# Macaron block with fp4 feed-forward: the last 64 features of the down product as a doubled float32r split

## Chip, cores and metric

One core of a Trainium2 chip. The metric is device time in microseconds of one execution of the whole program, median of repeated runs.

## What is computed

The input has 8 x 1024 tokens of 256 features, 8192 tokens in all. Six sublayers follow each other, each with a layer norm ahead of it and a residual sum behind it: fp4 feed-forward, attention with decay, fp4 feed-forward, ternary feed-forward, attention with memory, ternary feed-forward. The change lies in the fp4 feed-forward alone, which runs twice with the same weights:

```python
def fp4_quant_dequant(x):                      # blocks of 16 along the last dim
    xb = x.reshape(shape[:-1] + (shape[-1] // BLOCK, BLOCK))
    scale = jnp.maximum(jnp.max(jnp.abs(xb), axis=-1, keepdims=True) / 6.0, 1e-12)
    xn = xb / scale
    idx = jnp.searchsorted(_MID, jnp.abs(xn))
    return (_GRID[idx] * jnp.sign(xn) * scale).reshape(shape)

def fp4_linear(x, w):
    return jnp.einsum('bsk,nk->bsn', fp4_quant_dequant(x), fp4_quant_dequant(w))

gate = fp4_linear(x, w_gate)                   # 256 -> 704
y = fp4_linear(x, w_up)                        # 256 -> 704
h = jax.nn.silu(gate) * y
return fp4_linear(h, w_down)                   # 704 -> 256
```

## The kernel before

**Tiles.** Tokens are worked on in 64 tiles of 128 (`NT`), four to a group (`G`), 16 groups. The residual stream `X` stays on the chip for the whole program. `ffn_fp4(prepare, after)` is one fp4 stage. It runs `for i in range(NT + 3)`, a software pipeline by hand: iteration i makes the gate and up products of tile i, rounds tile i-1, multiplies the turned tile i-3 by its scales, and makes the down product of tile i-4.

**Order.** Nearly every instruction passes through `pin`, which ties it behind the instruction pinned before it on the same engine. So each engine runs in program order by itself, and instructions of different engines are held apart only by their data and by buffers that have to come free.

**One tile i, engine by engine.**
- PE: for each half q, two products of `pg` (gate) and two of `pu` (up), 128x352 each, in `products` (L861); the transpose `pts` of the scales of tile i-1 (L891) between `pg` and `pu` of the second half; then the down product `po` of tile i-4 (`down`, L960).
- ACT: silu of `pg` (L871), the copy of a scale (`copies`, L815) and the magnitudes of h (L821), the copy of the turned scales `sct` (L897).
- DVE: the rounding of tile i-1 to the fp4 grid (`round_grid`, L886: one instruction back into h, one that writes the grid values in bfloat16 into `gd`), the gate times up of tile i (`gated`, L876), the block maxima and reciprocals of `scale` (L804, L806, L811), layer norm statistics of the coming stage, the residual sum of `po` (L969).
- POOL (GpSimd): h times the reciprocal scales (`scale`, L817), and `multiplied` (L927): the turned grid of tile i-3 (`gt`) times its scales, which a DMA has spread into `ht`; in every second iteration also the normalized x of a coming group (`xt`), handled in the same way.
- SP issues the DMAs: `sd` takes the turned scales to memory (L899), `gt` is the DMA transpose of `gd` (L912), `ht` and `xt` spread the scales from `sd` (L904), `gtx` is the transpose of the rounded x (L1084).

There is one `gd`, two `gt`, one `sct`, and five `ht` in the first stage, four in the second. `pu` and `po` have one PSUM buffer each.

**The down product.** 704 features are five chunks of 128 and one of 64 (`DCH`, `NC` = 6). `ht` is [128, 6, 128] and `wd` [128, 6, 256], both float32; the unused 64 rows of the last chunk are zero, in `wd` and in `gd`. `down` makes six float32 products into `po`:

```python
for c in range(NC):
    kn = tail if c == NC - 1 else P
    pin(nc.tensor.matmul(po, lhsT=ht[:kn, c, :], rhs=wd[:kn, c, :],
                         start=(c == 0), stop=(c == NC - 1)))
```

**Weights and ends.** `w_down` is quantized during the first iterations of the first stage (`prep_down_scale`, `prep_down`) and turned in iteration 5 (`prep_down_turn`, L643 and L647), ahead of the first down product. The last two tiles of a stage don't go by DMA: `turn` (L948, L950) transposes h on PE in three groups of chunks, 4, 1 and 1, and ACT copies each group to `ht`.

**Elsewhere.** The ternary stages make their products from two float32r factors, a rounded high part and a remainder (`xh`, `xl` at L1193; `hh`, `hl` at L1220), against weights that stand as float32r.

Of the kernel before, what the change touches and what calls it, by code (L numbers as in the profile page):

```python
# [9 lines left out]
F32 = mybir.dt.float32  # L10
F32R = mybir.dt.float32r
BF16 = mybir.dt.bfloat16
I32 = mybir.dt.int32
AF = mybir.ActivationFunctionType
ALU = mybir.AluOpType
# [3 lines left out]
P = 128  # L19
D = 256  # L20
# [3 lines left out]
G = 4  # L24
# [10 lines left out]
FP4_TIE = 1.0 + 2.0**-22  # L35
# [4 lines left out]
def macaron_kernel(  # L40
# [25 lines left out]
    nc = tc.nc  # L66
    NB, S, _ = x.shape
# [3 lines left out]
    NI = w_gate.shape[0]  # L71
# [5 lines left out]
    DCH = [(k, min(P, NI - k)) for k in range(0, NI, P)]  # L77
# [365 lines left out]
    def turned_part(xt, k):  # L443
        return xt.rearrange("p (j k) t -> p k j t", k=2)[:, k]

    wd = w_f0.tile([P, NC, D], F32, name="wd")
    nc.gpsimd.memset(wd[DCH[-1][1] :, NC - 1, :], 0.0)
    with (
        tc.tile_pool(name="prep_ps", bufs=2, space=PSUM, side="right") as prep_ps,
        tc.tile_pool(name="prep_pq", bufs=1, space=PSUM, side="right") as prep_pq,  # L450
# [184 lines left out]
    def prep_down(c):  # L635
        fp4_round(wd_n[:, c, :], wd_sc.pop(c), raw, nc.gpsimd, pin)

    def prep_down_turn(ps, tag):
        for i, (k0, kn) in enumerate(DCH):
            pt = ps.tile([P, D], F32, tag=tag, name="ptd")  # L640
            for c in range(2):
                pin(
                    nc.tensor.transpose(  # L643
                        pt[:kn, c * P : (c + 1) * P], wd_n[:, c, k0 : k0 + kn], ident
                    )
                )
            pin(nc.scalar.copy(wd[:kn, i, :], pt[:kn, :]))  # L647


    def load_a0():  # L650
# [116 lines left out]
    def ffn_fp4(prepare, after):  # L767
        with ExitStack() as st:
# [10 lines left out]


            gd = gp.tile([P, NC * P], BF16, name="gd")
            nc.gpsimd.memset(gd[:, NI:], 0.0)
            scales = []
            for n in range(2):
                sc = gp.tile([P, P], F32, name=f"sc_{n}")
# [11 lines left out]
            DOWN = 5  # L797
            HT_BUFS = DOWN if prepare else 4

            def scale(v, pool, at, mul=nc.gpsimd, sc=None):  # L800
                vb = v.rearrange("p (b k) -> p b k", k=16)
                _, nb, _ = vb.shape
                am, sp = qp[:, at : at + nb], qp[:, at + nb : at + 2 * nb]
                pin(nc.vector.tensor_reduce(am, vb, AX.X, ALU.max, apply_absolute_value=True))  # L804
                pin(
                    nc.vector.tensor_scalar(  # L806
                        sp, am, -FP4_TIE / 6.0, -1e-12 * FP4_TIE, ALU.mult, ALU.min
                    )
                )
                rs = pool.tile([P, nb], F32, tag="q_rs", name="q_rs")  # L810
                pin(nc.vector.reciprocal(rs, sp))  # L811
                if sc is None:
                    sc = pool.tile([P, nb], F32, tag="q_sc", name="q_sc")
                copies.append(
                    lambda: pin(nc.scalar.activation(sc, sp, AF.Copy, scale=-1.0 / FP4_TIE))  # L815
                )
                pin(mul.tensor_tensor(vb, vb, rs[:, :, None].to_broadcast([P, nb, 16]), ALU.mult))  # L817
                return sc

# [61 lines left out]
            def by_dma(i):  # L881
                return 0 <= i < NT - 2

            def round_grid(v, mg, grid):
                for op, dst in ((ALU.add, v), (ALU.subtract, grid)):
                    pin(nc.vector.scalar_tensor_tensor(dst, mg, FP4_LEAST, v, ALU.max, op))  # L886
# [38 lines left out]
            def multiplied(wide, grid):  # L925
# [4 lines left out]
                    )  # L930
                )

            def scaled_turn(i):
                hs.pop(i)
                ht = spreading.pop(i)
                multiplied(ht, turning.pop(i))
                hts[i] = (ht, P)

            def turn(i):
                h, _ = hs.pop(i)  # L940
                ht = hp.tile([P, NC, P], F32, tag="ht", name="ht", bufs=HT_BUFS)
                for c0, c1 in ((0, 4), (4, 5), (5, 6)):
                    kn = DCH[c0][1]
                    pa = ps_t.tile([P, 4, P], F32, tag="pt", name="pt")
                    for c in range(c0, c1):
                        k0 = DCH[c][0]
                        pin(
                            nc.tensor.transpose(pa[:kn, c - c0, :], h[:, k0 : k0 + kn], ident)  # L948
                        )
                    pin(nc.scalar.copy(ht[:kn, c0:c1, :], pa[:kn, : c1 - c0, :]))  # L950
                hts[i] = (ht, DCH[-1][1])

            def down(i, ps=ps_o, tag="po"):
                g, j = divmod(i, G)
                ht, tail = hts.pop(i)
                po = ps.tile([P, D], F32, tag=tag, name="po")
                for c in range(NC):
                    kn = tail if c == NC - 1 else P
                    pin(
                        nc.tensor.matmul(  # L960
                            po,
                            lhsT=ht[:kn, c, :],
                            rhs=wd[:kn, c, :],
                            start=(c == 0),
                            stop=(c == NC - 1),
                        )
                    )
                pin(
                    nc.vector.scalar_tensor_tensor(  # L969
                        X[g][:, j, :], po, 0.5, X[g][:, j, :], ALU.mult, ALU.add  # L970
                    )
                )
# [38 lines left out]
            for i in range(NT + 3):  # L1011
                g, j = divmod(i, G)
                h = hp.tile([P, NI], F32, tag="h", name="h") if i < NT else None
                if i == 0 and not prepare:
                    xts[0], copied = turn_products(xts[0])
                    copied()
                pts = None
                for q in range(2):
                    if i < NT:
                        pg = ps_h.tile([P, NHALF], F32, tag="pg", name="pg", bufs=1)  # L1020
                        if q == 0:
                            pu = ps_h.tile([P, 2, 512], F32, tag="pu", name="pu", bufs=1)
                            sg = hp.tile([P, 2, NHALF], F32, tag="sg", name="sg", bufs=1)
                        products(i, q, 0, pg)
                        if q == 1 and i == 3:
                            xts[1], copied = turn_products(xts[1][0])
                        if prepare and late_weights and q == 1:
                            late_weights.pop()(ps_t)
                        if q == 1 and by_dma(i - 1):
                            pts = scales_turned(i - 1)  # L1030
                        products(i, q, 1, pu[:, q, 0:NHALF])
                        silu(sg, q, pg)
                        if i == NT - 1:
                            gated(h, sg, pu, slice(q, q + 1))
                        elif q:
                            gated(h, sg, pu, slice(0, 2))
                    if q == 0:
                        while copies and i < NT:
                            copies.pop(0)()
                    elif i == 3:  # L1040
                        copied()

                    if 0 < i < NT and q == 0:
                        magnitudes(hs[i - 1][0], qp[:, 0:NI])
                        if by_dma(i - 1):
                            round_grid(hs[i - 1][0], qp[:, 0:NI], gd[:, :NI])
                    if i == NT - 1:
                        if q == 1:
                            round_(*hs[i - 1], qp[:, 0:NI])

                        part = h[:, q * NHALF : (q + 1) * NHALF]
                        at = NI + q * NHALF // 8
                        mul = nc.vector if q else nc.gpsimd
                        halves.append((part, scale(part, hp, at, mul)))
                    if i == NT:
                        copies.pop(0)()
                        part, sc = halves.pop(0)
                        if q == 0:
                            mg2 = ps_h.tile([P, 2, 512], F32, tag="pu", name="mg", bufs=1)
                        mg = mg2[:, q, 0:NHALF]  # L1060
                        magnitudes(part, mg)
                        round_(part, sc, mg, nc.vector if q else nc.gpsimd)
# [6 lines left out]
                if 0 < i < NT:  # L1069

                    ln.advance(i - 1, 1)
                if by_dma(i - 3):
                    scaled_turn(i - 3)
                for key in list(xgrids):
                    gt, at = xgrids[key]
                    if at == i - 2:
                        xgrids.pop(key)
                        to_m, half_m = key
                        multiplied(xts[to_m][:, G * half_m : G * half_m + G, :], gt)
                for to_, half_ in list(xgrids):  # L1080
                    gx, at = xgrids[to_, half_]
                    if at == i - 1:
# [11 lines left out]
                if i < NT:  # L1094
                    own = scales[i % 2] if by_dma(i) else None
                    if own is not None:
                        scale(h, hp, NI, sc=own[:, : NI // 16])
                        hs[i] = (h, own)
                    else:
                        hs[i] = (h, scale(h, hp, NI) if i < NT - 1 else None)  # L1100
# [22 lines left out]
                    if NT - 18 <= i < NT - 2:  # L1123
                        begin(after, NT - 2 - i)
                if prepare and i == DOWN:
                    prep_down_turn(ps_t, "pt")
                if i >= DOWN or not prepare:
                    first = downs
                    while downs <= (i - 4 if i < NT else i - 3) and downs < first + 2:
# [976 lines left out]
```

## Time and profile before

| | us |
|---|---|
| median of 3 runs | 2589.17 (2587.45 to 2592.93) |
| the profiled execution, by its own time | 2594.43 |
| its span, first to last instruction | 2592.7 |
| PE busy | 2506.9 |
| DVE busy | 2087.8 |
| ACT busy | 1235.1 |
| POOL busy | 900.9 |
| first fp4 stage, first to last down product | 92 to 552 |
| second fp4 stage, first to last down product | 1028 to 1491 |

The page comes from one execution, whose own time stands beside its span. Busy time of PE counts from the start of a record to its modelled end, and records overlap, so what a product costs in a row of them is the distance from start to start. PEld is the loading of the stationary factor, which runs beside the products. A line of a timeline gives start, length, engine, line of the kernel, operation, what is written and read, sizes, count, and in brackets the idle time of the engine before it with what ended it. The granted clock of PE was full nearly throughout (mean 0.993).

### The profile page before, as it was taken

The numbers are of one execution on the slowest core, as the hardware profiler recorded it, in microseconds if no ns is written. First come the engines' busy times: TensorE is split into PE (matmuls) and PEld (weight loads), VectorE is DVE, ScalarE is ACT, GpSimd is POOL, SyncE is SP. The second block draws the span as 40 slices with busy tenths as digits, with TensorE's granted clock in tenths as the row PEclk, the third lists the DMA queues.
The fourth block names the chain that finished last, engine by engine and source line by source line (L and its number), as shares of the span: only waits on it lengthen the run. The fifth ranks groups of instructions, "written<-read, shape, count | busy, mean of one in ns | idle before, by whom it ended". The sixth has DMA issues, their size and how long they took to land.

```text
span 2592.7 us, 52415 instructions
## 1 busy us (share of the span) xinstructions
PE 2506.9 (97%) x20426; PEld 1868.6 (72%) x20426; DVE 2087.8 (81%) x4808; ACT 1235.1 (48%) x2785; POOL 900.9 (35%) x895
## 2 busy tenths in 40 slices
PE   4899999999999999999999999999999999999999
PEld 2577777766666666777777689995677776778998
DVE  7898888758878778988888599647888888879864
ACT  5344444334333333444444276656555555437664
POOL 4565555521101003555555300004555555530000
PEclk9899999999999999999999999999999999999999
DMA  7455556500000002556555300000000000000001
GB/s 218 87 117 115 113 118 116 107 23 18 10 22 14 2 2 48 114 116 115 117 116 113 66 1 1 1 1 1 2 2 2 2 2 2 2 2 26 33 33 41
DMA packets 199897, 132.40 MB, mean 51 GB/s; under 512 B 138048, under 2 KB 174944, under 8 KB 199648
## 3 DMA queue, kind: packets, MB, share of 16 engines
q1 hardware_dynamic: 198704, 127.85, 22.8%
q8 instruction: 161, 2.64, 0.4%
q0 software_dynamic: 240, 0.54, 0.1%
q14 instruction: 88, 0.72, 0.1%
q10 hardware_dynamic: 704, 0.66, 0.1%
HBM read 80.77 MB, written 16.52 MB: 38 GB/s over the span
## 4 chain that ended last, share of the span: by engine, by line
PE 84%; DVE 11%; ACT 2%; issue 1%; DMA 1%; POOL 1%; SPq 0%; DVEq 0%; POOLq 0%; ACTq 0%
PE po L960 11%; PE pu L861 10%; PE pg L861 10%; PE po L1220 9%; PE ph L1193 9%; PE sc L1263 5%; PE py L1347 5%; PE pq L1361 4%; PE pkv L1361 4%; PE po L1361 4%; PE pk L1361 4%; PE py L1329 2%; PE pmo L1786 2%; DVE at L1272 1%; DVE qp L804 1%
## 5 line engine op out<-in xcount | busy, mean ns | idle before, releaser
L960 PE MATMUL po<-wd,ht 128*128 128x256 f32 x1536 | 358.1, 383 | 0.6 <-DVE x L969 0.5
L861 PE MATMUL pu<-wgu,xt 128*128 128x352 f32 x1024 | 349.6, 464 | 8.3 <-DVE h L876 7.9
L861 PE MATMUL pg<-wgu,xt 128*128 128x352 f32 x1024 | 348.8, 463 | 4.4 <-ACT sg L871 4.1
L960 PEld LDWEIGHTS po<-wd,ht 128*128 128x128 f32 x1536 | 294.6, 193 | 62.4 <-issue 2.2
L871 ACT ACTIVATE sg<-pg 128x352 f32<-128x352 f32 x256 | 118.1, 461 | 451.5 <-PE pg L861 422.6
L817 POOL TENSOR_TENSOR h<-h,q_rs 128x704 f32<-128x704 f32 (+1 forms) x128 | 176.2, 1376 | 413.1 <-DVE q_rs L811 413.1
L861 PEld LDWEIGHTS pu<-wgu,xt 128*128 128x128 f32 x1024 | 186.5, 193 | 112.3 <-issue 19.6
L861 PEld LDWEIGHTS pg<-wgu,xt 128*128 128x128 f32 x1024 | 195.0, 191 | 97.8 <-ACT sg L871 9.2
L1220 PE MATMUL po<-w,hl 128*128 128x256 f32 x1024 | 243.7, 280 | 1.4 <-DVE hl L1204 1.2
L1220 PE MATMUL po<-w,hh 128*128 128x256 f32 x1024 | 243.3, 280 | 0.0
L1902 POOL TENSOR_TENSOR mo<-mo 128x256 f32<-128x256 f32 x192 | 164.2, 855 | 196.6 <-DVE mo L1799 188.1
L927 POOL TENSOR_TENSOR ht<-gt,ht 128x768 f32<-128x768 bf16 x124 | 205.7, 1659 | 0.0
L1193 PE MATMUL ph<-xh,w 128*128 128x512 f32 x512 | 204.4, 401 | 1.4 <-ACT hf L1201 0.6
L1193 PE MATMUL ph<-xl,w 128*128 128x512 f32 x512 | 201.8, 395 | 0.0
L1204 DVE TENSOR_TENSOR hl<-hf,hh 128x512 fp32r<-128x512 f32 x256 | 168.3, 684 | 39.4 <-ACT hh L1202 35.9
L1220 PEld LDWEIGHTS po<-w,hl 128*128 128x128 f32 x1024 | 192.1, 188 | 4.5 <-DVE hl L1204 2.5
L1220 PEld LDWEIGHTS po<-w,hh 128*128 128x128 f32 x1024 | 192.1, 188 | 2.6 <-DVE x L1228 0.3
L1201 ACT ACTIVATE hf<-ph,b1c 128x512 f32<-128x512 f32 x256 | 168.0, 695 | 18.5 <-PE ph L1193 16.1
L1272 DVE TENSOR_TENSOR at<-sc,dec 128x512 f32<-128x512 f32 x256 | 158.6, 682 | 11.8 <-PE sc L1263 11.8
L886 DVE SCALAR_TENSOR_TENSOR h<-qp,h 128x704 f32<-128x704 f32 x124 | 110.2, 889 | 69.1 <-ACT qp L821 68.9
L1272 DVE TENSOR_TENSOR at<-sc,tri 128x512 f32<-128x512 f32 x256 | 164.9, 679 | 0.4 <-PE sc L1263 0.4
L1202 ACT CAST hh<-hf 128x512 fp32r<-128x512 f32 x256 | 149.2, 628 | 17.0 <-PE po L1220 15.2
(276 smaller groups left out, 5303.0 us busy)
## 6 DMA issues: line engine op xcount, KB each, us to landing
ht<-sd SPq DMA_DIRECT2D x124, 384.0 KB
xt<-sd SPq DMA_DIRECT2D x56, 256.0 KB
sd<-sct SPq DMA_DIRECT2D x124, 64.0 KB
x<-in_x SPq DMA_DIRECT2D x15, 512.0 KB
out<-x SPq DMA_DIRECT2D x15, 512.0 KB
t_raw<-in_w_t SPq DMA_DIRECT2D x16, 256.0 KB
gt<-gd SPq DMA_TRANSPOSE x124
gtx<-xn SPq DMA_TRANSPOSE x56
```

Of the source, the lines that this page charges most:

```text
L817: pin(mul.tensor_tensor(vb, vb, rs[:, :, None].to_broadcast([P, nb, 16]), ALU.mult))
L861: nc.tensor.matmul(ps, lhsT=xts[g][:, 2 * j + k, :], rhs=wgu[:, k, (2 * q + of_up) * NHALF : (2 * q + of_up + 1) * NHALF], start=(k == 0), ...
L927: nc.gpsimd.tensor_tensor(wide.rearrange("p c t -> p (c t)"), grid.rearrange("p c t -> p (c t)"), wide.rearrange("p c t -> p (c t)"), ALU. ...
L960: nc.tensor.matmul(po, lhsT=ht[:kn, c, :], rhs=wd[:kn, c, :], start=(c == 0), stop=(c == NC - 1),)
L1193: nc.tensor.matmul(ph, lhsT=w1[:, k, f * P : (f + 1) * P], rhs=xt[:, k, :], start=(k == 0 and xt is xh), stop=(k == 1 and xt is xl),)
L1201: nc.scalar.activation(hf, ph, AF.Gelu, bias=b1c[:, f : f + 1])
L1202: nc.scalar.copy(hh[:, f, :], hf)
L1204: nc.vector.tensor_tensor(hl[:, f, :], hf, hh[:, f, :].bitcast(F32), ALU.subtract)
L1220: nc.tensor.matmul(po, lhsT=ht[:, f, j * P : (j + 1) * P], rhs=w2[:, f, :], start=(f == 0 and ht is hh), stop=(f == NF - 1 and ht is hl),)
L1272: nc.vector.tensor_tensor(at, sc.rearrange("p m (e t) -> p (m e) t", e=2), weight, ALU.mult)
L1361: nc.tensor.matmul(dst, lhsT=lhsT, rhs=rhs, start=n == 0, stop=n == len(parts) - 1)
L1902: summed = nc.gpsimd.tensor_tensor(mo[:, :, :, 0, :], mo[:, :, :, 0, :], mo[:, :, :, m, :], ALU.add)
```

## The change

The last 64 features are taken out of the float32 product and stand twice, so that they fill a chunk of 128.

- Weights: `ws` (float32r) holds in its first 64 rows the rounded last 64 rows of the turned down weights, and in the other 64 the remainder. For this `prep_down_turn` has POOL copy the last 64 columns of `wd_n` twice into `wt`, transposes that, and has ACT write the rounded copies `wh` and `ws[:64]` and DVE the difference `ws[64:]`.
- Left factor: the grid in `gd` is doubled by a POOL copy (`gd[:, NI:]`), and the scales of the last four blocks by a second, 4-wide ACT copy (`tail`), so the last chunk of `ht` holds the 64 features twice. `split` makes on POOL its rounded part `hh` and the remainder `hl`, both float32r.
- `down` makes five float32 products and then `hh` against `ws` and `hl` against `ws`.
- The two multiplications by scales (`scaled_turn`, and `multiplied` for xt) move from the end of iteration i to ahead of its products.
- For the last two tiles `turn` has POOL copy the 64 features twice into `hd` and transposes in two groups of three chunks.
- The two zero fills (`wd`, `gd`) go.

```diff
+        spare = pool.tile([P, G, D], F32, tag="xn1", name="wt", bufs=1)
+        wt = spare[:, 0, :].rearrange("p (c n k) -> p c n k", c=2, n=2)
+        for c in range(2):
+            pin(nc.gpsimd.tensor_copy(
+                    wt[:, c], wd_n[:, c, None, NI - NK :].to_broadcast([P, 2, NK])))
...
+                wh = spare[:, 1, :].bitcast(F32R)
+                pin(nc.scalar.copy(wh, pt))
+                pin(nc.scalar.copy(ws[:NK], pt[:NK]))
+                pin(nc.vector.tensor_tensor(
+                        ws[NK:], pt[NK:], wh[NK:].bitcast(F32), ALU.subtract))
...
+                copies.append(lambda: copied(0, nb, 0))
+                if tail:
+                    copies.append(lambda: copied(nb, nb + tail, tail))
...
+            def split(ht):
+                hh = hp.tile([P, P], F32R, tag="hh", name="hh", bufs=3 if prepare else 2)
+                pin(nc.gpsimd.tensor_copy(hh, ht[:, NC - 1, :]))
+                hl = hp.tile([P, P], F32R, tag="hl", name="hl", bufs=3 if prepare else 2)
+                pin(nc.gpsimd.tensor_tensor(
+                        hl, ht[:, NC - 1, :], hh.bitcast(F32), ALU.subtract))
+                return hh, hl
...
             def scaled_turn(i):
                 multiplied(ht, turning.pop(i))
-                hts[i] = (ht, P)
+                hts[i] = (ht, *split(ht))
...
+                hd = lnp.tile([P, G, D], F32, tag="xn1", name="hd", bufs=1)[:, 0, 0:P]
+                pin(nc.gpsimd.tensor_copy(hd[:, 0:NK], h[:, NI - NK :]))
+                pin(nc.gpsimd.tensor_copy(hd[:, NK:], h[:, NI - NK :]))
-                for c0, c1 in ((0, 4), (4, 5), (5, 6)):
+                for c0, c1 in ((0, 3), (3, NC)):
...
-                for c in range(NC):
+                factors = [(ht[:, c, :], wd[:, c, :]) for c in range(NC - 1)]
+                factors += [(hh, ws), (hl, ws)]
+                for n, (left, right) in enumerate(factors):
...
+                if by_dma(i - 3):
+                    scaled_turn(i - 3)
+                for key in list(xgrids):
+                    ...
+                        multiplied(xts[to_m][:, G * half_m : G * half_m + G, :], gt)
                 for q in range(2):
...
                             round_grid(hs[i - 1][0], qp[:, 0:NI], gd[:, :NI])
+                            pin(nc.gpsimd.tensor_copy(gd[:, NI:], gd[:, NI - NK : NI]))
...
-                if by_dma(i - 3):
-                    scaled_turn(i - 3)
...
-                        scale(h, hp, NI, sc=own[:, : NI // 16])
+                        scale(h, hp, NI, sc=own, tail=NK // 16)
...
-                    prep_down_turn(ps_t, "pt")
+                    prep_down_turn(ps_t, "pt", lnp)
```

More of the change, by code (lines that the diff above doesn't have):

```diff
@@ L444, in turned_part @@
         return xt.rearrange("p (j k) t -> p k j t", k=2)[:, k]
-    wd = w_f0.tile([P, NC, D], F32, name="wd")
-    nc.gpsimd.memset(wd[DCH[-1][1] :, NC - 1, :], 0.0)
+    NK = DCH[-1][1]
+    wd = w_f0.tile([P, NC - 1, D], F32, name="wd")
+    ws = w_f0.tile([P, D], F32R, name="ws")
     with (
@@ L636, in prep_down, with prep_down_turn @@
         fp4_round(wd_n[:, c, :], wd_sc.pop(c), raw, nc.gpsimd, pin)
-    def prep_down_turn(ps, tag):
-        for i, (k0, kn) in enumerate(DCH):
+    def prep_down_turn(ps, tag, pool):
+        spare = pool.tile([P, G, D], F32, tag="xn1", name="wt", bufs=1)
+        wt = spare[:, 0, :].rearrange("p (c n k) -> p c n k", c=2, n=2)
+        for c in range(2):
+            pin(
+                nc.gpsimd.tensor_copy(
+                    wt[:, c], wd_n[:, c, None, NI - NK :].to_broadcast([P, 2, NK])
+                )
+            )
+        for i, (k0, _) in enumerate(DCH):
             pt = ps.tile([P, D], F32, tag=tag, name="ptd")
             for c in range(2):
-                pin(
-                    nc.tensor.transpose(
-                        pt[:kn, c * P : (c + 1) * P], wd_n[:, c, k0 : k0 + kn], ident
+                if i < NC - 1:
+                    part = wd_n[:, c, k0 : k0 + P]
+                else:
+                    part = wt[:, c].rearrange("p n k -> p (n k)")
+                pin(nc.tensor.transpose(pt[:, c * P : (c + 1) * P], part, ident))
+            if i < NC - 1:
+                pin(nc.scalar.copy(wd[:, i, :], pt))
+            else:
+                wh = spare[:, 1, :].bitcast(F32R)
+                pin(nc.scalar.copy(wh, pt))
+                pin(nc.scalar.copy(ws[:NK], pt[:NK]))
+                pin(
+                    nc.vector.tensor_tensor(
+                        ws[NK:], pt[NK:], wh[NK:].bitcast(F32), ALU.subtract
                     )
                 )
-            pin(nc.scalar.copy(wd[:kn, i, :], pt[:kn, :]))
     def load_a0():
@@ L781, in ffn_fp4 @@
             gd = gp.tile([P, NC * P], BF16, name="gd")
-            nc.gpsimd.memset(gd[:, NI:], 0.0)
             scales = []
@@ L798, in ffn_fp4, with scale @@
             HT_BUFS = DOWN if prepare else 4
-            def scale(v, pool, at, mul=nc.gpsimd, sc=None):
+            def scale(v, pool, at, mul=nc.gpsimd, sc=None, tail=0):
                 vb = v.rearrange("p (b k) -> p b k", k=16)
@@ L813, in scale, with copied @@
                     sc = pool.tile([P, nb], F32, tag="q_sc", name="q_sc")
-                copies.append(
-                    lambda: pin(nc.scalar.activation(sc, sp, AF.Copy, scale=-1.0 / FP4_TIE))
-                )
+                def copied(c0, c1, back):
+                    pin(
+                        nc.scalar.activation(
+                            sc[:, c0:c1], sp[:, c0 - back : c1 - back], AF.Copy,
+                            scale=-1.0 / FP4_TIE,
+                        )
+                    )
+                copies.append(lambda: copied(0, nb, 0))
+                if tail:
+                    copies.append(lambda: copied(nb, nb + tail, tail))
                 pin(mul.tensor_tensor(vb, vb, rs[:, :, None].to_broadcast([P, nb, 16]), ALU.mult))
@@ L931, in multiplied @@
                 )
+            def split(ht):
+                hh = hp.tile([P, P], F32R, tag="hh", name="hh", bufs=3 if prepare else 2)
+                pin(nc.gpsimd.tensor_copy(hh, ht[:, NC - 1, :]))
+                hl = hp.tile([P, P], F32R, tag="hl", name="hl", bufs=3 if prepare else 2)
+                pin(
+                    nc.gpsimd.tensor_tensor(
+                        hl, ht[:, NC - 1, :], hh.bitcast(F32), ALU.subtract
+                    )
+                )
+                return hh, hl
             def scaled_turn(i):
@@ L941, in turn @@
                 ht = hp.tile([P, NC, P], F32, tag="ht", name="ht", bufs=HT_BUFS)
-                for c0, c1 in ((0, 4), (4, 5), (5, 6)):
-                    kn = DCH[c0][1]
-                    pa = ps_t.tile([P, 4, P], F32, tag="pt", name="pt")
-                    for c in range(c0, c1):
[L946 to L951, printed above, removed]
+                hd = lnp.tile([P, G, D], F32, tag="xn1", name="hd", bufs=1)[:, 0, 0:P]
+                pin(nc.gpsimd.tensor_copy(hd[:, 0:NK], h[:, NI - NK :]))
+                pin(nc.gpsimd.tensor_copy(hd[:, NK:], h[:, NI - NK :]))
+                for c0, c1 in ((0, 3), (3, NC)):
+                    pa = ps_t.tile([P, 3, P], F32, tag="pt", name="pt")
+                    for c in range(c0, c1):
+                        part = h[:, c * P : (c + 1) * P] if c < NC - 1 else hd
+                        pin(nc.tensor.transpose(pa[:, c - c0, :], part, ident))
+                    pin(nc.scalar.copy(ht[:, c0:c1, :], pa[:, : c1 - c0, :]))
+                hts[i] = (ht, *split(ht))
             def down(i, ps=ps_o, tag="po"):
                 g, j = divmod(i, G)
-                ht, tail = hts.pop(i)
+                ht, hh, hl = hts.pop(i)
                 po = ps.tile([P, D], F32, tag=tag, name="po")
-                for c in range(NC):
-                    kn = tail if c == NC - 1 else P
+                factors = [(ht[:, c, :], wd[:, c, :]) for c in range(NC - 1)]
+                factors += [(hh, ws), (hl, ws)]
+                for n, (left, right) in enumerate(factors):
                     pin(
                         nc.tensor.matmul(
[L961 to L965, printed above, removed]
+                            po, lhsT=left, rhs=right, start=(n == 0), stop=(n == NC)
                         )
@@ L1017, in ffn_fp4 @@
                 pts = None
+                if by_dma(i - 3):
+                    scaled_turn(i - 3)
+                for key in list(xgrids):
+                    gt, at = xgrids[key]
+                    if at == i - 2:
+                        xgrids.pop(key)
+                        to_m, half_m = key
+                        multiplied(xts[to_m][:, G * half_m : G * half_m + G, :], gt)
                 for q in range(2):
@@ L1071, in ffn_fp4 @@
                     ln.advance(i - 1, 1)
-                if by_dma(i - 3):
-                    scaled_turn(i - 3)
[L1074 to L1079, printed above, removed]
                 for to_, half_ in list(xgrids):
```

## The prediction

> **What bounds the kernel now.** I read the page's busy times and chain first, then the waits of PE in the second fp4 stage, then the timeline of one tile of that stage.
>
> ```profile
> span 2592.7 us, 52415 instructions
> PE 2506.9 (97%) x20426; PEld 1868.6 (72%) x20426; DVE 2087.8 (81%) x4808; ACT 1235.1 (48%) x2785; POOL 900.9 (35%) x895
> ...
> PE 84%; DVE 11%; ACT 2%; issue 1%; DMA 1%; POOL 1%; SPq 0%; DVEq 0%; POOLq 0%; ACTq 0%
> PE po L960 11%; PE pu L861 10%; PE pg L861 10%; PE po L1220 9%; PE ph L1193 9%; PE sc L1263 5%; PE py L1347 5%; PE pq L1361 4%; PE pkv L1361 4%; PE po L1361 4%; PE pk L1361 4%; PE py L1329 2%; PE pmo L1786 2%; DVE at L1272 1%; DVE qp L804 1%
> ...
> L960 PE MATMUL po<-wd,ht 128*128 128x256 f32 x1536 | 358.1, 383 | 0.6 <-DVE x L969 0.5
> ```
>
> The product that is changed, L960, is the largest line of the chain. Its 1536 records are 2 stages x 64 tiles x 6 chunks x 2: a float32 product is two records on PE. Now the fp4 stage by windows (columns: stretch, length, busy of PE, PEld, DVE, ACT, POOL, clock, DMA share, GB/s), and PE's and POOL's waits there:
>
> ```profile
> 1200.00:1400.00 200.00, 200.00 (x782) 144.92 (x781) 168.31 (x322) 84.96 (x214) 111.23 (x82) 1.00 0.58 115
> ```
>
> ```profile
> PE pu L861 <- DVE h L876: 2.4, 3, 1.4
> ```
>
> ```profile
> POOL h L817 <- DVE q_rs L811: 187.0, 59, 5.9
> POOL xt L927 <- DMA gtx<-xn: 10.7, 18, 1.8
> ```
>
> PE is busy through the whole stretch; in 440 us (1000 to 1440) it waited for DVE 3 times. POOL waited 187.0/59 = 3.2 us per tile for DVE. So time on PE in these stages is time of the kernel. One tile on PE:
>
> ```profile
> 1103.17 1.35 PE L861 MATMUL pu<-wgu,xt 128*128 128x352 f32 x4
> 1104.35 2.75 PE L960 MATMUL po<-wd,ht 128*128 128x256 f32 x12
> 1106.94 1.35 PE L861 MATMUL pg<-wgu,xt 128*128 128x352 f32 x4
> ```
>
> The next such pu starts at 1110.60: a tile takes 7.43 us, of which the 12 records of po take 1106.94 - 1104.35 = 2.59, 215.8 ns each from start to start. (The 383 ns of the page is one record's own length; records overlap.)
>
> **The product: two float32 records out, two float32r records in.** The last chunk's float32 product (2 x 215.8 = 431.6 ns) goes; two products of float32r factors, hh and hl against ws, come. That form runs in the ternary stages, same shape and also two left factors in turn:
>
> ```profile
> 1702.37 0.28 PE L1220 MATMUL po<-w,hh 128*128 128x256 f32 x1
> 1702.49 0.28 PE L1220 MATMUL po<-w,hl 128*128 128x256 f32 x1
> ...
> 1709.79 0.28 PE L1220 MATMUL po<-w,hl 128*128 128x256 f32 x1
> 1709.91 1.03 PE L1174 MATMUL pt<-ident,xn 128*128 128x128 f32 x8
> ```
>
> 64 records in 7.54 us: 117.8 ns each, one record a product. Per tile 431.6 - 235.6 = 196.0 ns less; 128 tiles: -25.1 us. Bounds: at best one record is half a float32 record, 107.9 ns, which makes it -27.6. At worst the two new waits for POOL ahead of hh and hl are not hidden: PE's sequencer shows a semaphore wait at 51 ns each in L960's rows, so 128 x 0.102 = 13.1 us are lost and -12.0 is left. I take 117.8, because L960's first product already waits for POOL and DVE and starts one pu interval after the last pu, 296 ns, as if there were no wait. A switch from float32 to float32r costs nothing visible either: the first float32r product starts 28 ns after the last transpose and the next 320 later, together 348, where 109 + 233 = 342 is the sum of the two ordinary intervals.
>
> **POOL: three instructions more per tile.** hl is a two-operand 128x128: L668, the same form, takes 456 ns. hh is a 128x128 cast: L475 takes 289. The 64-wide copy into gd lies between a 128x64 memset (154) and a 64-wide scaling (328); I take 240. Sum 0.985 us; if both copies cost as L476 (658, a 128x128 scaling) it is 1.77. POOL goes from 111.23/26.9 = 4.14 us a tile to 5.12 (5.91) of 7.24. The place that matters is the tile with an xt product, every second one. There POOL had 1.31 us left before h (0.37 more went to waiting for gtx), as the timeline of its chain shows:
>
> ```profile
> 1095.74 1.66 POOL L927 TENSOR_TENSOR ht<-gt,ht 128x768 f32<-128x768 bf16 x1
> 1097.56 0.88 DVE L876 TENSOR_TENSOR h<-sg,pu 128x704 f32<-128x704 f32 x1
> 1097.76 1.16 POOL L927 TENSOR_TENSOR xt<-gtx,xt 128x512 f32<-128x512 bf16 x1 [0.37 <-DMA gtx<-xn]
> 1099.64 0.43 DVE L811 RECIPROCAL q_rs<-qp 128x44 f32<-128x44 f32 x1
> 1100.22 1.39 POOL L817 TENSOR_TENSOR h<-h,q_rs 128x704 f32<-128x704 f32 x1 [1.31 <-DVE q_rs L811]
> 1101.64 0.76 ACT L821 ACTIVATE qp<-h 128x704 f32<-128x704 f32 x1 [0.19 <-POOL h L817]
> 1103.18 0.88 DVE L886 SCALAR_TENSOR_TENSOR h<-qp,h 128x704 f32<-128x704 f32 x1
> 1104.90 0.88 DVE L876 TENSOR_TENSOR h<-sg,pu 128x704 f32<-128x704 f32 x1
> ```
>
> 1.68 spare covers 0.985, and 1.77 less the shorter tile's 0.2 by a hair not. What is late then is h, ACT's magnitudes, DVE's rounding and the gate L876; behind the gate waits pu of the next tile, at 1100.69, 2.26 us after the gate's end at 1098.43. So even an uncovered 0.3 us costs nothing on PE: cost 0.
>
> **DVE beside a busier POOL.** The gd rounding lasted 891 to 893 ns in all 124 cases, with POOL busy half the time: nothing shows that POOL slows DVE. SBUF — State Buffer, Who interferes with whom, in the Trainium skill speaks against more GpSimd work: a DVE instruction with two SBUF inputs is blocked by a GpSimd instruction that reads SBUF. Here qp, pu and po lie in PSUM, so DVE's long instructions have one SBUF input, and the rule, read to the end, also gives 0; had they two, up to 0.985 us a tile would be added to DVE's 6.26.
>
> **The queues.** The multiplication of ht and xt, moved ahead of the tile's products, issues no DMA, and on POOL it stands where it stood, since each engine's order is kept by itself; only hh, hl and gd's tail come between. gd's tail holds the transpose of the grid on SP: with an xt product it ends about 1097.40 + 0.75 + 1.16 + 0.24 = 1099.55, so the transpose issues 1.85 us later than 1097.70, and behind it on SP wait the two spreads of scales; the next issue before them, sd at 1103.90, still finds SP free (1.24 + 0.1 + 0.6 + 0.6 after 1099.55 is 1102.1). The spread ht is read two tiles later, at 1110.0, after an issue at 1101 instead of 1099; 384 KB at the 115 GB/s of the window take 3.4 us. Cost 0. ACT gains a 4-wide copy a tile (L815's least, 0.18 us), between the scale's copy, over at 1101.45, and the magnitudes at 1101.64: it just fits, and PE's transpose that needs it comes at 1103.06. Cost 0; without that cover it is 0.2 us in the same chain, under the same 2.26.
>
> **Start and ends.** In the first stage the last transposes of the down weights wait for POOL's doubled copy, behind the fifth tile's h: ht from 87.06, then 1.66 + 0.75 + 1.16 + 0.24 + 1.39 + 2 x 0.29 is 92.9, plus two transposes 93.3, against 92.24 for the first po: +1.1 us. At the end of each stage POOL copies the tail twice before the second group of transposes, so the products of the two tiles before it start about 0.9 us later (538.5 for 537.63); but the last tile's transposes, which take from 544.30 to 545.71 in three groups with a wait for ACT between, can run back to back in two, 6 x 0.109 = 0.65: 0.9 - 0.76 = +0.15 a stage (bounds -0.8, +0.9), 0.3 in all. Some 13 early tiles of both stages have the gate 0.9 us or more behind PE, and once PE waited 0.67 for it (123.48): there DVE, not PE, sets the pace. Up to 13 x 0.196 = 2.5 us of the saving is lost there; I take 1.0.
>
> **Sum.** -25.1 + 1.1 + 0.3 + 1.0 = -22.7. The profiled execution took 2594.43 (span 2592.7 and 1.7 around it), 5.3 above the median of 2589.17. It would take 2571.7; the median run 2566.5.
>
> **Rivals.** *A: DVE takes over.* The tile above took DVE 7.34 us from gate to gate, with no idle time worth naming; the new PE tile is 7.24. If every second tile stays at 7.34 and the others can't make up for it, 64 x 0.1 = 6.4 are lost; with all early tiles (2.5 instead of 1.0) and half of the waits' 13.1 it is -22.7 + 6.4 + 1.5 + 6.5 = -8.3: 2580.9. For it: DVE at 84% already. Against it: the light tiles take 6.8 from gate to gate at least (0.88, 0.9, 0.21, 0.43, 1.39, 0.76, 1.77 and handovers), so lateness is made up, and 2.26 us of it cost nothing. *B: POOL becomes the bound, and the kernel slower.* Two tiles hold 2 x (1.39 + 1.66) + 1.16 + 1.06 = 8.3 us of POOL in 14.87; it decides from (14.87 - 8.3)/2 = 3.3 us of new work a tile, three times my price. At 3.6 a tile lasts 7.76, 118 tiles are 0.33 longer: +39, 2628. Only casts to float32r that run in a slow way of their own would do it; no POOL row shows such a cast. *C: no gain on PE*, the mixed float32r records at 215.8: 0 + 1.1, 2590.
>
> **How the numbers follow.** Forecast (2561 to 2572) 0.78; A (2572 to 2584) 0.13; C 0.03; B 0.06. One measurement of this kernel tells some 0.2%, 5.2 us, from no change. Faster 0.91, same 0.03, slower 0.06. The range goes from the cheapest records with the best stage ends, -27.6 + 1.1 - 1.6 = -28.1, or 2561, less 1 for the scatter of the runs (they lay 1.7 under to 3.8 over the median), to the middle of A (2577).
>
> **What would show it.** Right: the down line with ten records of 216 ns a tile and two of 118; tiles of 7.24 us; POOL near 70% in the stage, still waiting for DVE before h; PE's waits in 1000 to 1440 under 5 us. Wrong: gaps before the hh or hl records, a POOL that never waits, the gate's end within 0.1 us of the next pu through the stage, or a float32r record over 150 ns.

## The result, and the profile after

| | before | changed | ratio, 95% interval |
|---|---|---|---|
| median, same chip | 2588.31 us | 2652.86 us | 1.0247 [1.0225, 1.0269] |
| range | 2585.21 to 2592.93 (4 runs) | 2648.49 to 2656.14 (4 runs) | |
| profiled execution, span | 2594.43, 2592.7 | 2653.02, 2651.3 | |

The changed kernel is slower by 64.5 us where 22.7 less was forecast. The page of the changed kernel: span, busy times, shares of the chain.

```profile
span 2651.3 us, 53038 instructions
PE 2499.9 (94%) x20426; PEld 1847.5 (70%) x20426; DVE 2080.4 (78%) x4809; ACT 1239.4 (47%) x2906; POOL 1021.8 (39%) x1282
...
PE 59%; DVE 15%; DMA 8%; issue 6%; POOL 6%; ACT 3%; SPq 0%; POOLq 0%; DVEq 0%; ACTq 0%
```

PE and DVE are a little less busy than before, and no engine is fuller than PE. But PE holds 59% of the chain instead of 84%, and DMA and POOL, which had 1% each, hold 8% and 6%: the chain now runs in part through transfers. The second fp4 stage by windows (stretch, length, busy PE, PEld, DVE, ACT, POOL, clock, DMA share, GB/s) and PE's waits from 1000 to 1500:

```profile
1260.00:1460.00 200.00, 186.37 (x729) 129.37 (x727) 154.21 (x301) 80.16 (x224) 126.89 (x152) 1.00 0.66 108
```

```profile
PE pts L919 <- ACT sc L836: 14.6, 17, 1.2
PE pg L889 <- ACT sg L899: 10.0, 6, 4.0
PE pu L889 <- DVE h L904: 8.0, 10, 1.3
```

PE, full before, idles 13.6 us in 200 at full clock, behind ACT's scales and silu and DVE's gate. POOL is busy 63% there: it isn't the bound by its load. By the starts of the gate times up (L904 on DVE, "the gate" from here on) in the timeline, tiles 8 to 62 take 432.2 and 432.1 us in the two stages, 8.00 us a tile, for 401.0 and 402.5 before: 60.8 of the 64.5 us. POOL's groups by form, first the line of before, then three of the changed kernel:

```profile
L927 POOL TENSOR_TENSOR xt<-gtx,xt 128x512 f32<-128x512 bf16 x56 | 65.1, 1163 | 22.3 <-DMA gtx<-xn 17.4 <-issue 2.6 <-PE pu L861 1.8
```

```profile
L955 POOL TENSOR_TENSOR xt<-gtx,xt 128x512 f32<-128x512 bf16 x56 | 65.1, 1163 | 134.7 <-DMA gtx<-xn 134.6
...
L967 POOL TENSOR_TENSOR hl<-ht,hh 128x128 fp32r<-128x128 f32 x128 | 58.4, 456 | 10.3
...
L964 POOL CAST hh<-ht 128x128 fp32r<-128x128 f32 x128 | 37.1, 290 | 26.8 <-ACT ht L990 11.2 <-PE po L1001 7.6
```

The new instructions cost what was estimated. The line that changed is an old one: POOL now idles 134.7 us ahead of the multiplication of xt, nearly all of it for the transfer gtx, instead of 22.3. Why gtx is late stands in SP's issues (start, length, engine, line, what). Before, one cycle of two tiles:

```profile
1092.77 1.20 SPq L1084 DMA_TRANSPOSE gtx<-xn  x1
1096.47 0.58 SPq L899 DMA_DIRECT2D sd<-sct  x1
1097.70 1.23 SPq L912 DMA_TRANSPOSE gt<-gd  x1
1099.04 0.59 SPq L904 DMA_DIRECT2D ht<-sd  x1
1099.68 0.58 SPq L904 DMA_DIRECT2D xt<-sd  x1
1103.90 0.57 SPq L899 DMA_DIRECT2D sd<-sct  x1
1105.05 1.24 SPq L912 DMA_TRANSPOSE gt<-gd  x1
1106.39 0.59 SPq L904 DMA_DIRECT2D ht<-sd  x1
1107.04 1.20 SPq L1084 DMA_TRANSPOSE gtx<-xn  x1
```

After, with those rows of POOL, PE and ACT in the same stretch that matter here; the rows between them are left out:

```profile
1204.38 1.20 SPq L1122 DMA_TRANSPOSE gtx<-xn  x1
...
1210.40 1.16 POOL L955 TENSOR_TENSOR xt<-gtx,xt 128x512 f32<-128x512 bf16 x1 [3.72 <-DMA gtx<-xn]
1211.50 0.24 POOL L1092 COPY gd<-gd 128x64 bf16<-128x64 bf16 x1
1211.69 1.38 POOL L845 TENSOR_TENSOR h<-h,q_rs 128x704 f32<-128x704 f32 x1
1211.77 1.93 SPq L940 DMA_TRANSPOSE gt<-gd  x1
...
1212.76 2.32 PE L1001 MATMUL po<-wd,ht 128*128 128x256 f32 x10
1213.11 0.76 ACT L849 ACTIVATE qp<-h 128x704 f32<-128x704 f32 x1 [3.19 <-POOL h L845]
1213.81 0.61 SPq L932 DMA_DIRECT2D ht<-sd  x1
...
1214.52 0.58 SPq L932 DMA_DIRECT2D xt<-sd  x1
1215.03 0.28 PE L1001 MATMUL po<-ws,hl 128*128 128x256 f32 x1
1215.15 1.34 PE L889 MATMUL pg<-wgu,xt 128*128 128x352 f32 x4
1215.15 0.58 SPq L927 DMA_DIRECT2D sd<-sct  x1
...
1216.15 1.24 SPq L940 DMA_TRANSPOSE gt<-gd  x1
...
1221.25 0.59 SPq L932 DMA_DIRECT2D ht<-sd  x1
1221.89 1.20 SPq L1122 DMA_TRANSPOSE gtx<-xn  x1
```

Read it as a ring, a chain of waits that comes back to its start. POOL's tail copy (the last 64 columns of `gd`, L1092) stands behind the multiplication of xt, which waits for gtx; so gt can't issue before 1211.77, and ht and xt go behind it, 640 KB of spreads. The next sd issues at 1215.15, 0.6 us behind xt instead of 4.2. Its 128 packets, which took 0.4 us in one row before, now run in two halves, 64 from 1216.4 to 1216.8 and 64 from 1219.9 to 1220.6, and SP stands at the next ht, which reads sd, until 1221.25. Behind that ht on SP is the next gtx: 1221.89. It lands late, xt's multiplication waits again (1226.84), and so round. This turn takes 17.5 us for two tiles; the median over 1060 to 1460 is 15.72 from one gtx to the next, for 14.86 before. In the 25 tiles of that stretch in which sd follows an xt, its last packet ends 5.2 us after its issue, for 1.6 before (medians of the trace's packet times). What reaches PE comes off the ring at POOL: h (1211.69) is behind the late xt, then ACT's magnitudes (3.19 us idle), DVE's rounding, and the gate, whose end PE's next pu waits for. SP's own waits from 1060 to 1460, before and then after, show the two links:

```profile
SPq L899 <- ACT xn L317: 101.7, 24, 4.5
SPq L899 <- ACT mgx L821: 93.7, 25, 4.8
```

```profile
SPq L940 <- POOL gd L1092: 125.8, 49, 5.9
SPq L932 <- DMA sd<-sct: 73.0, 25, 3.9
```

Before, SP stood idle for its next sd, behind ACT; now it stands ahead of gt, for the tail copy, and ahead of ht, for sd.

### The profile page after: what moved, and what is told of

Read it like the earlier page. It is cut to its first block, busy times and chain, and to the rows that moved or that the text cites. A ratio compares the mean times of both kernels' runs of the same rounds, so it can differ in the third digit from the quotient of the medians.

```text
span 2651.3 us, 53038 instructions
## 1 busy us (share of the span) xinstructions
PE 2499.9 (94%) x20426; PEld 1847.5 (70%) x20426; DVE 2080.4 (78%) x4809; ACT 1239.4 (47%) x2906; POOL 1021.8 (39%) x1282
## 4 chain that ended last, share of the span: by engine, by line
PE 59%; DVE 15%; DMA 8%; issue 6%; POOL 6%; ACT 3%; SPq 0%; POOLq 0%; DVEq 0%; ACTq 0%
PE po L1258 9%; PE ph L1231 8%; PE sc L1301 5%; PE py L1385 4%; DMA gtx<-xn 4%; PE pq L1399 4%; PE pkv L1399 4%; PE pk L1399 4%; PE po L1399 4%; PE po L1001 3%; DMA sd<-sct 3%; POOL h L845 3%; DVE qp L823 3%; PE pu L889 2%; PE py L1367 2%
## 5 line engine op out<-in xcount | busy, mean ns | idle before, releaser
L1001 PE MATMUL po<-wd,ht 128*128 128x256 f32 x1280 | 304.5, 386 | 0.7 <-DVE x L1006 0.6
L1001 PEld LDWEIGHTS po<-wd,ht 128*128 128x128 f32 x1280 | 247.3, 194 | 55.4 <-issue 2.5
L889 PEld LDWEIGHTS pg<-wgu,xt 128*128 128x128 f32 x1024 | 187.0, 192 | 114.4 <-ACT sg L899 31.7
L1524 POOL TENSOR_TENSOR x<-x,ob 128x1024 f32<-128x1024 f32 x16 | 37.9, 2366 | 332.2 <-ACT xn L317 310.1
```

The lines of the kernel that those rows point to most:

```text
L889: nc.tensor.matmul(ps, lhsT=xts[g][:, 2 * j + k, :], rhs=wgu[:, k, (2 * q + of_up) * NHALF : (2 * q + of_up + 1) * NHALF], start=(k == 0), ...
L1001: nc.tensor.matmul(po, lhsT=left, rhs=right, start=(n == 0), stop=(n == NC))
```

## Experiments

Theory W is the ring of waits just read. Its first rival is L: the load itself, that is 0.98 us more of POOL in a tile, or what that does to DVE, wherever it stands. The table gives medians, and ratios to the kernel before on the same chip.

| run | us | ratio, 95% interval |
|---|---|---|
| e1 xt back behind the products | 2577.80 | 0.9943 [0.9928, 0.9957] |
| e2 tail copy on DVE | 2588.13 | 0.9985 [0.9976, 0.9995] |
| e3 gtx issued first | 2585.47 | 0.9982 [0.9973, 0.9992] |
| e4 before, with tail copy and move | 2647.23 | 1.0210 [1.0195, 1.0226] |
| e5 before, with the move | 2589.61 | 0.9998 [0.9989, 1.0007] |
| e6 changed, without the move | 2621.43 | 1.0121 [1.0107, 1.0135] |
| e7 e1 and hl made twice | 2577.56 | 0.9948 [0.9932, 0.9963] |
| e8 e1 and hd by ACT | 2571.28 | 0.9930 [0.9918, 0.9943] |
| e9 changed, sd issued by ACT | 2652.85 | 1.0240 [1.0223, 1.0257] |
| e10 e8 and gtx issued first | 2575.66 | 0.9947 [0.9932, 0.9961] |

**e1: the ring cut at POOL.** The multiplication of xt goes back behind the products, so that the tail copy no longer stands behind it:

```diff
                 if by_dma(i - 3):
                     scaled_turn(i - 3)
-                for key in list(xgrids):
-                    ...multiplied(xts[to_m][...], gt)
                 for q in range(2):
...
+                for key in list(xgrids):
+                    ...multiplied(xts[to_m][...], gt)
                 for to_, half_ in list(xgrids):
                     ...gtx...
```

> Edit: only the multiplication of xt goes back behind the tile's products, so that on POOL gd's tail copy stands ahead of it; every instruction of the change stays. Theory W (a ring of waits: gd's tail copy stands behind the xt product, which waits for the transfer gtx; the transpose gt waits on SP for that copy; the spreads behind gt come late; the next sd lands behind them, and ht and the next gtx wait on SP for sd): the ring is cut, 2561 to 2575 us, POOL's waits for gtx under 30 us in all instead of 135. Theory L (POOL's load: three more instructions a tile make h late): POOL has the same work, 2630 to 2655 us.

2577.80, faster than before, though 3 over the top of what W expected. The same work on the same engines, in another order on one of them, is 75 us apart. POOL's line of e1:

```profile
L955 POOL TENSOR_TENSOR xt<-gtx,xt 128x512 f32<-128x512 bf16 x56 | 65.3, 1166 | 15.9 <-DMA gtx<-xn 15.8
```

**e2: the tail copy off POOL.** `nc.gpsimd.tensor_copy(gd[:, NI:], ...)` becomes `nc.vector.tensor_copy`.

> Edit: only gd's tail copy goes from POOL to DVE, where it stands right behind the rounding that it reads. W: SP waits for DVE alone, as before the change, the ring is cut: 2561 to 2580 us (DVE has a short copy more a tile). L: POOL loses 0.24 of some 1.0 us of its new work a tile, so most of the loss stays: 2625 to 2650 us.

2588.13: the ring is gone (POOL's idle ahead of xt 7.5 us, SP's waits for sd 8.8), but the time is 8 us above what W expected, and 10 above e1. The copy takes DVE 235 ns where POOL took 237. The first eight gate intervals of the first stage take 83.9 us where e1 takes 77.4, and tiles 8 to 62 of both stages together 4.7 us more than in e1. That a copy more on DVE costs this, because DVE sets the pace in those tiles, is a reading that no further run tests.

**e3: the ring cut at SP.** The issue of gtx goes ahead of the tile's sd, gt and ht; the tail copy stays behind xt.

```diff
                 if pts is not None:
+                    for to_, half_ in list(xgrids): ...gtx...
                     spread(i - 1, pts)
...
-                for to_, half_ in list(xgrids): ...gtx...
```

> Edit: only the issue of the transpose gtx moves on SP, ahead of sd, gt and ht of its tile, so that it no longer waits for sd's landing. W: the ring is cut at another place, the xt product finds gtx landed and gd's tail copy is not held: 2561 to 2600 us. L: nothing changes for POOL: 2640 to 2660 us.

2585.47, as W expected. Its POOL line and SP's waits from 1060 to 1460:

```profile
L955 POOL TENSOR_TENSOR xt<-gtx,xt 128x512 f32<-128x512 bf16 x56 | 65.3, 1166 | 0.0
```

```profile
SPq L932 <- DMA sd<-sct: 78.3, 32, 4.4
SPq L940 <- POOL gd L1092: 60.6, 35, 2.6
```

SP waits for sd as long as in the changed kernel, and yet 67 us are gone: the wait costs mainly through gtx, queued behind it. Of the 7.7 us that e3 takes more than e1, 7.3 lie in tiles 8 to 62; what makes them stays open.

**e4, e5: one part alone on the kernel before.** e4 adds to it the tail copy and the move of both multiplications, e5 the move only; in both the products stay as before.

```diff
+                if by_dma(i - 3):
+                    scaled_turn(i - 3)
+                for key in list(xgrids): ...multiplied...
                 for q in range(2):
...
+                            pin(nc.gpsimd.tensor_copy(gd[:, NI:], gd[:, NI - 64 : NI]))   # e4 alone
...
-                if by_dma(i - 3):
-                    scaled_turn(i - 3)
-                for key in list(xgrids): ...multiplied...
```

> Edit on the kernel before: only gd's tail copy on POOL and the move of the two multiplications ahead of the products are added; the down product, its factors and PE's work stay as before (the doubled grid meets scales of zero). W: the ring closes with 0.24 us of new POOL work a tile, 2605 to 2655 us. L: within 10 us of the kernel before, 2588 to 2600 us.

> Edit on the kernel before: only the two multiplications move ahead of the tile's products; no tail copy, no split, PE's work as before. W (the tail copy behind the xt product closes the ring): without the copy nothing on SP waits for the xt product, 2585 to 2597 us, no change. Rival M (the move itself does it): 2630 us or more.

2647.23 and 2589.61. Together with the move, a copy of 0.24 us on an engine that was busy 56% of the stretch (111.23 of 200 us) makes the kernel 56 us slower, without hh, hl, or any change on PE; the move by itself costs nothing. Tiles 8 to 62 take 432.2 and 427.3 us in e4, close to the 432.2 and 432.1 of the changed kernel, and SP's waits are much the same:

```profile
SPq L912 <- POOL gd L1055: 122.1, 51, 4.6
SPq L904 <- DMA sd<-sct: 64.3, 25, 3.6
```

**e6: the change without the move,** the multiplications back at the end of the iteration, behind the tail copy.

> Edit on the changed kernel: neither multiplication moves, so POOL copies gd's tail first, waiting for DVE's rounding, and multiplies and splits ht and multiplies xt after it. W: SP's transpose waits for the tail copy, but that stands ahead of the xt product, so no ring: 2570 to 2590 us, some us more than with xt alone moved back, since POOL's multiplications start about 2 us later. L: as the changed kernel or slower, 2645 us or more.

A miss: 2621.43 for 2570 to 2590. The waits of the first ring are gone (SP's for sd 1.5 us, POOL's for gtx 1.1), but another closes. POOL from 1204, and its waits from 1060 to 1460:

```profile
1204.26 0.24 POOL L1084 COPY gd<-gd 128x64 bf16<-128x64 bf16 x1 [1.87 <-DVE gd L914]
1204.45 1.65 POOL L955 TENSOR_TENSOR ht<-gt,ht 128x768 f32<-128x768 bf16 x1
1206.17 0.29 POOL L964 CAST hh<-ht 128x128 fp32r<-128x128 f32 x1
1206.54 0.46 POOL L967 TENSOR_TENSOR hl<-ht,hh 128x128 fp32r<-128x128 f32 x1
1206.95 1.16 POOL L955 TENSOR_TENSOR xt<-gtx,xt 128x512 f32<-128x512 bf16 x1
1208.07 1.39 POOL L845 TENSOR_TENSOR h<-h,q_rs 128x704 f32<-128x704 f32 x1
1212.16 0.24 POOL L1084 COPY gd<-gd 128x64 bf16<-128x64 bf16 x1 [2.71 <-DVE gd L914]
```

```profile
POOL gd L1084 <- DVE gd L914: 118.5, 51, 2.7
POOL h L845 <- DVE q_rs L830: 6.5, 8, 1.5
```

The tail copy waits for the rounding of one tile, and ht, hh, hl, xt and h of the next tile stand behind it; h feeds ACT's magnitudes (0.76) and the rounding (0.89 + 0.89), which the next tail copy waits for. The ring's parts add up to 0.24 + 1.65 + 0.29 + 0.46 + 1.16 + 1.39 + 0.76 + 1.78 = 7.73 and, without xt, 6.57; tail copies stand 7.90 and 6.96 apart. The mean of these two, 7.43, is 0.19 over the 7.24 that PE's work in a tile would take. Tiles 8 to 62 take 413.3 us in each stage, 7.65 a tile; the other 0.22 were not followed up. So of these versions the good one has the ht multiplication ahead of the tail copy, and the harm is in moving xt's along with it.

**e7: more load, no other order.** e1, with the subtraction that makes hl issued twice, 0.46 us of POOL a tile.

> Edit on the kernel with xt's product moved back: POOL makes hl twice, 0.46 us more a tile, and nothing else changes. W (POOL has room once the ring is cut): within 8 us of that kernel, 2576 to 2586 us. L (POOL's time is the price): 118 tiles by 0.46 us, some 54 us more, 2625 to 2635 us.

2577.56, against 2577.80 for e1 (ratios 0.9948 and 0.9943): L has fallen. POOL, with 1.44 us a tile more than before, costs no time that can be seen, as long as the tail copy doesn't stand behind the late xt.

**e8: the last two tiles.** In e1, PE's longest single wait of a stage is at its end, for POOL's copies into hd, 3.4 us in each stage. In e8 ACT makes them (`nc.gpsimd.tensor_copy(hd...)` becomes `nc.scalar.copy(hd...)`). PE's waits for hd in e1, and then in e8, from 1000 to 1500:

```profile
PE pt L989 <- POOL hd L984: 3.4, 1, 3.4
```

```profile
PE pt L989 <- ACT hd L984: 1.7, 1, 1.7
```

> Edit on the kernel with xt's product moved back: the doubled copies for the last two tiles of a stage are made by ACT and not by POOL. With it PE no longer waits 3.4 us at each stage's end for POOL's copy: if that wait is on the path, 4 to 6 us less, 2571 to 2574 us; if something else is late behind it, the same 2578.

2571.28: 19.5 us under before, the lowest median of all versions. The first stage's wait falls from 3.4 to 1.8. By the ratios e8 is some 3.4 us under e1, which is what the two shorter waits add up to; but the two intervals overlap, so the gain itself isn't shown beyond the noise. Against e7, on the same chip, it is 6.3 us, and the waits for hd, 3.9 us in each stage of e7, explain 4.3 of them.

**e9: a queue of its own for sd.** In the changed kernel, `nc.sync.dma_start(out=sd...)` becomes `nc.scalar.dma_start(out=sd...)`.

> The changed kernel with one thing different: the small transfer sd (64 KB) is issued by ACT instead of SP, so that it stands in no queue behind the spreads ht and xt. Theory W (ring; the link is sd's place behind the late spreads in one queue): sd lands within about 1 us of its issue, SP's waits for sd in 1060 to 1460 fall from 73.0 us to under 20, gtx issues earlier, and most of the loss is gone: 2565 to 2605. Rival S (the DMA engines themselves are shared, and sd has to wait for the spreads' packets whichever queue it is in): SP's waits for sd stay at 50 us or more and the time at 2630 to 2655. Rival G (the wait for gtx holds by itself, sd is only a companion): waits for sd are gone, but POOL's waits for gtx stay at 50 us or more and the time at 2625 to 2655.

2652.85: nothing changed, and the link as W had it ("sd's place behind the late spreads in one queue") is wrong; the result is the one that rival S named. The queues of e9 (packets, MB, share of 16 engines' span) and SP's waits from 1060 to 1460:

```profile
q1 hardware_dynamic: 180848, 119.71, 22.7%
q10 hardware_dynamic: 18560, 8.79, 2.1%
```

```profile
SPq L940 <- POOL gd L1092: 168.0, 48, 6.9
SPq L932 <- DMA sd<-sct: 75.7, 25, 4.1
```

sd did move to another queue, q10, and lands no earlier. ACT issued one at 1214.02, 0.6 us behind SP's xt (1213.43). Of its 128 packets of 512 bytes, 64 ran from 1215.3 to 1215.6 and 64 from 1218.2 to 1219.0, about when the last of xt's 2048-byte packets were through (1218.8). Over 1060 to 1460 an sd that follows an xt takes 5.3 us to its last packet, for 5.2 in the changed kernel. So the queue isn't what holds sd. That the DMA engines which carry the spreads hold it fits these times, but no run takes the spreads away from them.

**e10: what is left of gtx's wait.** e8 with e3's edit.

> The version with the xt multiplication behind the tail copy and the last two tiles' doubled copies on ACT, and also gtx issued ahead of the tile's spreads on SP. If what is left of the wait for gtx (15.8 us of POOL in all) still costs PE something in the early or the last tiles of a stage, it takes 2563 to 2570; if PE is full there already and the rest of the missing 3 us lies at the stage ends and in the start, no difference: 2569 to 2574. Over 2578 would mean that sd, now issued later behind gtx, holds PE.

2575.66: POOL's wait for gtx is 0.0, and nothing is gained over e8 (the intervals overlap). It lies between the two cases named; whether it is slower than e8 is open. Taking away what is left of the wait for gtx (12.3 us in e8) gained nothing here. Whether it would without a later sd stays open too: SP's wait for sd grows from 20.3 us in e8 to 47.0 (1060 to 1460).

## Why the prediction was wrong

- **The step that failed: "The queues", "Cost 0".** It saw that the tail copy would stand behind xt and hold gt, ht and xt back by 1.85 us, and then looked at two things only: that "sd at 1103.90 still finds SP free", and that ht is read two tiles later. That an issue finds its queue free says nothing of when it lands: behind the late spreads sd took 5.2 us from its issue to its last packet, for 1.6 before. The profile of before had no room for a delay here. The sd issued at 1103.90 began its packets at 1105.13, 1.23 us after the issue, as one with nothing ahead of it did (1096.47, 1097.70), and xt's last packet had ended just then, at 1105.13. The estimate of 3.4 us also counted the 384 KB of ht alone, without the 256 KB of xt. And what stands behind the next ht on SP, gtx, was not asked for, nor that gtx is what the copy's predecessor waits for. The delay of 1.85 us was taken as one delay; it feeds back into its own cause, and tiles 8 to 62 became 60.8 us longer where nothing was counted. This is shown by e1 and e3, each of which cuts the ring at one place, and by e4 and e5, of which e4 closes it without hh, hl or the new products, and e5, without the tail copy, doesn't.
- **"The multiplication of ht and xt ... on POOL it stands where it stood"** is true of the old instructions among themselves (e5: no difference), but false for the new one: what counts is that the tail copy comes behind xt (changed kernel, e4) or ahead of ht (e6). Each of the two places closes a ring of its own; the place between them (e1) closes none.
- **PE's term was right.** The down product starts at 1212.76 and the next pg at 1215.15: 2.39 us for 2.59. Where the rings are cut and PE sets the pace, in most tiles of e8 from the 25th on, the gate's interval is 7.24, as worked out; before it was 7.43 to 7.44.
- **POOL's terms were right:** 290 + 456 + 237 = 0.983 us for 0.985. Its cover was not: "1.68 spare" ahead of h held 0.37 of waiting for gtx, and that wait grew to 134.7 us in all. Spare time that ends with a transfer isn't fixed.
- **DVE beside POOL: right.** gd's rounding in the timeline after takes 0.89 us.
- **The early tiles were undersized,** "I take 1.0" and the bound of 2.5 too. In e8 the first 24 intervals of the gate take 196.0 and 176.0 us in the two stages, for 197.5 and 177.6 before: 1.5 and 1.6 saved where 24 x 0.196 = 4.7 each were at stake, so 6.3 lost. In the first four tiles of a stage the gate ends 0.05 us ahead of the pu that waits for it, as it did before: there DVE sets the pace and a shorter product moves nothing. Behind those the gate is 0.8 us or more ahead in most tiles, and what keeps the saving away is not shown.
- **The stage ends were undersized:** "+0.15 a stage", and PE waited 3.4 us for POOL's hd in each stage of e1. ACT's copies in e8 bring that to 1.8 and 1.7.
- **The rivals:** A and C were not what happened. B, the slower case, had the wrong mechanism: POOL has room (e7), and the point that it named, 3.3 us of new work, was never near. A rival by order in a queue rather than by load was missing.
- **Where the forecast would have stood** without the ring: -22.7 with 6.3 for the early tiles instead of 1.0 is -17.4. e1, with every instruction of the change, measured -13.5, and e8 -19.5. The wait, and not the size of the saving, decided the result.

## What to carry to other kernels

A new instruction on an engine that works in a fixed order is priced by its place there, and its length alone can mislead (e4: 0.24 us a tile cost 56; e7: 1.44 us a tile cost nothing): list what stands ahead of it there and what that waits for, and what stands behind the transfer that it releases in the issuing engine's queue, until the list ends or comes back to itself. If it comes back, the time of one turn with its handovers against the cycle (in e6 7.43 us between tail copies on the mean of two tiles, against 7.24) is the number to compare, not the engine's idle time. An issue with ample time can go ahead of one that has to wait, where the wait is on a ring (e3; in e10, without the ring, it gained nothing). That a small transfer which others wait for should not follow big ones is suggested by sd's times; no run here sends it ahead of them.

## What the runs showed of the hardware

A queue of its own gave a small transfer no precedence here: issued by ACT into q10, sd landed as late behind 640 KB of spreads from SP's queue as when it stood in that queue (5.3 and 5.2 us from issue to last packet, SP's waits for it 75.7 and 73.0 us). A copy of a 128x64 bfloat16 tile costs the same on POOL and on DVE, 237 and 235 ns.
